# An adaptive-norm layer with a state-space mixer and a routed expert layer: vector copies issued by ScalarE, and the first batch's norm ordered first behind products with the streamed identity

## The chip, the core and the metric

The kernel runs on one core of one Trainium2 chip. The core has five queues of instructions that run in order, each on its own: TensorE (PE in the profile; its weight loads are PEld), VectorE (DVE), ScalarE (ACT), GpSimd (POOL) and SyncE (SP, which here only issues DMAs). The metric is the time of one execution on the device in microseconds (us).

## The reference

The input `x` is 8 batches of 512 tokens with 256 features, all in float32. From a vector `c` per batch six modulation vectors are made; then a mixer and an expert layer are added to `x`:

```python
mod = (silu(c) @ wmod).reshape(8, 6, 1, 256)
sa, ca, ga, sb, cb, gb = (mod[:, i] for i in range(6))
ga, gb = (sign(g) * max(|g|, 0.25) for g in (ga, gb))
h = layernorm(x) * (1 + ca) + sa
x = x + ga * mixer(h)
h = layernorm(x) * (1 + cb) + sb
x = x + gb * experts(h)

def mixer(x):            # 512 inner channels, 16 states, 4 taps
    xz = layernorm(x, gamma, beta) @ W_in.T
    x_part, z = split(xz)
    x_conv = silu(causal_conv4(x_part) + conv_b)
    state_t = state_{t-1} @ A.T + x_part_t @ Bm.T        # over 512 tokens
    y_t = (x_conv_t + state_t @ Cm) * sigmoid(z_t)
    return x + y @ W_out.T

def experts(x):          # 8 experts, hidden size 1024, each token goes to its top one
    probs = softmax(x @ wr + br); p1, p2 = top2(probs)
    return p1 / (p1 + p2) * (gelu(x @ w1[e] + b1[e]) @ w2[e] + b2[e])
```

## The kernel before, in words

**Two parts.** The first handles the mixer and the routing, batch by batch; it writes each token's row (features, statistics, gate) to a DRAM table `xp_d`, whose last 768 columns hold the second half of the modulation vectors for that token's batch, and scatters token numbers sorted by expert into `ids_d`. The second part gathers blocks of up to 256 tokens of one expert, loads that expert's weights, and computes the two expert products (`ph`, `py`).

**The planner.** Nothing is emitted directly. The class `Plan` stands in for the chip's engines: each call is noted with the data it reads and writes, an estimated length and a due time (`nc.due`). Then `order()` repeatedly picks, over all queues, the instruction that could start first, with the due time as the tie-break, and `emit()` writes the instructions in that order. So each engine's order is fixed in the program; an instruction that is placed early and has to wait holds up everything behind it on its engine. A DMA counts as 0.4 us of its issuing queue in these estimates (1.3 on POOL).

**The prologue** has three pieces, all spread over PE, DVE, ACT and POOL:

- `three()` makes one half of the modulation vectors by products with `wm` (tiles `pm`, `pg`), and a chain of seven small DVE operations (copies, `gate`, `mag`). It is called for the first batch alone, broadcast to all partitions (`bc0`), and by `vectors()` for all batches (`mod`, 8 partitions), whose results are stored to DRAM as `mod_d` and `modb_d`. `vectors()` also needs the same vectors with features on partitions (`modT`), from which it makes the router's weights (`rw`, `rg`, `psc`, `wo`, `pr`). Before, `modT` comes from 24 small products `pf` and its own small DVE operations.
- `states()` makes powers of the state matrix (`pa` on PE, copied to `at`), and from them `lt`, `cs` (through `pq`), `wb` (through `pw1`), `lm` (through `pm2`) and `bw` (through `pb`). The copies out of PSUM and between small tiles are on DVE.
- constants: `seen`, `sl_at` and `ex_at` are written by one-element memsets on POOL.

**One batch** is `stage_norm` (load `xt`, load the broadcast vectors `bc` from `mod_d`, two norms with `bn_stats`, `rs` on POOL, `nm` on DVE and `xn` on ACT, then transposes `tp_a` and ACT's copy to `xnT`), `stage_base` (POOL multiplies `h` and `wb_`, transposes `tp_b` to `baseT`), `stage_conv` (`pv`, the carries `pd_0` to `pd_2` over blocks of tokens, four projections `px` to `u` and `sv` on ACT and three taps each on DVE, then SiLU on ACT), `stage_out` (four more projections to `tz`, the state's output `pc`, the residual product `po` and the routing) and `stage_place` (rows to `xp_d`, sorting). `sv`, `u` and `tz` follow the projections; `pc` needs the last carry. PSUM pools: `ps_x` (tag `px`, three buffers), `ps_s` (one), `ps_t` (two), `ps_o` (two).

In `stage_place` the second half of the vectors is copied, 1.5 MB per batch, from `modb_d` to all 512 rows of the batch in `xp_d`. Before, SP issues these copies: two in batch 0, then one in each batch's stage.

```python
            for n in range(b + 1 if b else 0, min(b + 2, B)):
                nc.sync.dma_start(
                    out=xp_d[n * L : (n + 1) * L, OWN:ROW], in_=modb_d[n].partition_broadcast(L)
                )
```

In the profile nearly all instructions carry the line of `Plan.add` that calls the engine (L154 or L159), so they are told apart by their tiles. A product of float32 shows as two instructions (x2).

Of the kernel before, what the change touches and what calls it, by code (L numbers as in the profile page):

```python
# [10 lines left out]
FP = mybir.dt.float32  # L11
I32 = mybir.dt.int32
AF = mybir.ActivationFunctionType
ALU = mybir.AluOpType
# [21 lines left out]
class Plan:  # L36
# [20 lines left out]
    def __init__(self, tc, last=None):  # L57

        self.tc, self.nc = tc, tc.nc
        self.free = {q: last.free[q] if last else 0.0 for q in self.REACH}  # L60
        self.ops, self.touched, self.tiles = [], {}, {}
        self.due, self.also, self.pairing = 0.0, ([], []), 0
        for name in self.QUEUES:
            setattr(self, name, self.Engine(self, name))
# [71 lines left out]
    def add(self, name, op, args, kw):  # L136
# [12 lines left out]
        if queue == "PE" and last and last["queue"] == "PE" and (  # L149
            last["out"] == out.tensor.name or (self.pairing and last["pairing"] == self.pairing)  # L150
        ):

            me = last
            me["calls"].append(lambda: getattr(getattr(self.nc, name), op)(*args, **kw))  # L154
            me["length"] += 0.05 if self.pairing else length
        else:
            me = dict(
                i=len(self.ops), queue=queue, due=self.due,
                calls=[lambda: getattr(getattr(self.nc, name), op)(*args, **kw)],  # L159
                before=set(), after=set(), uses=set(), length=length + (0.3 if small else 0.0),  # L160
                size=0, out=out.tensor.name, pairing=self.pairing,
            )
            self.ops.append(me)
        if op == "activation":
            me["table"] = {AF.Gelu: 1, AF.Silu: 2, AF.Tanh: 2}.get(args[2] if len(args) > 2 else None)
# [25 lines left out]
    def order(self):  # L191
# [18 lines left out]
        done = [0.0] * len(ops)  # L210
        order, table = [], 2

# [12 lines left out]

        while len(order) < len(ops):
            best = None
            for q, l in ready.items():
                for o in l:
# [6 lines left out]
                    if best is None or (at, o["due"]) < best[:2]:  # L236
                        best = (at, o["due"], o)
            assert best is not None, "no buffer for any instruction that could be next"
            at, _, o = best
            table = o.get("table") or table  # L240

            for n in o["uses"] - held:
# [4 lines left out]
            ready[o["queue"]].remove(o)  # L247
            free[o["queue"]] = at + o["length"]
            end = at + o["length"]
            if o["size"]:  # L250
# [39 lines left out]
def adaln_mamba_moe_kernel(  # L290
# [88 lines left out]
    nc.gpsimd.memset(seen, 0.0)  # L379
    for e in range(E):  # L380
        nc.gpsimd.memset(seen[0:1, e : e + 1], float(e * TOK))
    run = cpool.tile([1, E], FP, name="run")


    sl_at = cpool.tile([1, 4, NSLOT], FP, name="sl_at")
    for i in range(NSLOT):
        single = i >= NPAIR
        m = i - NPAIR if single else i
        for q, v in enumerate((
            m, NPAIR + m // 2 if single else m, (m % 2) * P if single else 0,  # L390
            0 if single else NSING,
        )):
            nc.gpsimd.memset(sl_at[:, q, i : i + 1], float(v))

    ex_at = cpool.tile([1, 2, 2 * E], FP, name="ex_at")
    for e in range(2 * E):
        nc.gpsimd.memset(ex_at[:, 0, e : e + 1], float(e % E))
        nc.gpsimd.memset(ex_at[:, 1, e : e + 1], float((e % E) * TOK))

# [32 lines left out]
    with tc.tile_pool(name="wa", bufs=1) as wa, tc.tile_pool(  # L432
# [81 lines left out]
        def vectors():  # L514

            nc.due = 2.5 * PERIOD
            for half, to in ((0, mod_d), (1, modb_d)):
                mod = wa.tile([B, 3, D], FP, name=f"mod{half}", tag="mod")
                three(mod, sT, half, B)
                nc.sync.dma_start(out=to, in_=mod.rearrange("b i d -> b (i d)"))  # L520
            nc.due = 1e6


            pf = ps_o.tile([P, 6, B], FP, name="pf", tag="po")
            for m in range(6):
                w, at_m = (wmh[1], m) if m < 4 else (wmh[0], m)
                for k in range(KD):
                    nc.tensor.matmul(
                        pf[:, m], lhsT=w[:, k, at_m * P : (at_m + 1) * P],
                        rhs=sT[:, k, :], start=(k == 0), stop=(k == KD - 1),  # L530
                    )
            nc.vector.tensor_copy(modT[:, 0:2], pf[:, 0:2])
            nc.vector.tensor_scalar(modT[:, 2:4], pf[:, 2:4], 1.0, None, ALU.add)
            gT = modT[:, 4:6]
            nc.vector.tensor_copy(gT, pf[:, 4:6])
            mT = wa.tile([P, KD, B], FP, name="mT")
            nc.vector.scalar_tensor_tensor(mT, gT, -1.0, gT, ALU.mult, ALU.max)
            nc.vector.tensor_scalar(mT, mT, 0.25, None, ALU.max)
            nc.vector.tensor_scalar(gT, gT, 0.0, 2.0, ALU.is_ge, ALU.mult)
            nc.vector.scalar_tensor_tensor(gT, gT, -1.0, mT, ALU.add, ALU.mult)  # L540

# [51 lines left out]
        def states():  # L593


            for j in range(STEPS - 1):
                pa = ps_s.tile([DS, 2, DS], FP, name="pa", tag="ps")
                for s in range(2):
                    nc.tensor.matmul(
                        pa[:, s], lhsT=at[:, j, 1 - s], rhs=at[:, j, s], start=True, stop=True  # L600
                    )
                nc.vector.tensor_copy(at[:, j + 1], pa)
            i16 = ident[0:DS, 0:DS]
            a3t = wa.tile([DS, DS], FP, name="a3t")
            pa3 = ps_s.tile([DS, DS], FP, name="pa3", tag="ps")
            nc.tensor.matmul(pa3, lhsT=at[:, 0, 1], rhs=at[:, 1, 0], start=True, stop=True)
            nc.vector.tensor_copy(a3t, pa3)
            power = [i16, at[:, 0, 0], at[:, 1, 0], a3t, at[:, 2, 0]]
# [5 lines left out]
            for i in range(CH):  # L614
                for j in range(i + 1):
                    nc.vector.tensor_copy(lt[:, i, j * SP : j * SP + DS], power[i - j])
                nc.vector.tensor_copy(
                    lt[:, i, :].rearrange("p (q r) -> p q r", r=SP)[:, :, DS:],
                    power[i + 1].unsqueeze(1).to_broadcast([DS, CH, DS]),
                )  # L620
# [8 lines left out]
            for i, (l, r) in enumerate((  # L629
# [3 lines left out]
                nc.tensor.matmul(pmo[:, i], lhsT=l, rhs=r, start=True, stop=True)  # L633
            nc.vector.tensor_copy(more[:, 0:5], pmo)
            pm28 = ps_s.tile([DS, DS], FP, name="pm28", tag="ps")
            nc.tensor.matmul(pm28, lhsT=at[:, 4, 0], rhs=more[:, 0], start=True, stop=True)
            nc.vector.tensor_copy(more[:, 5], pm28)
# [8 lines left out]
            nc.vector.tensor_copy(wb[:, :, DS:], pw1)  # L646

# [4 lines left out]
            for j, m in enumerate(gaps):  # L652
                nc.vector.tensor_copy(
                    lx[:, j, :].rearrange("p (q r) -> p q r", r=SP)[:, :, DS:],
# [3 lines left out]
            nc.vector.memset(ix, 0.0)  # L658
            nc.vector.tensor_copy(ix[:, DS:], i16)
            pm2 = ps_s.tile([P, len(gaps), 2 * DS], FP, name="pm2", tag="ps")  # L660
# [3 lines left out]
            nc.vector.tensor_copy(lm, pm2)  # L664

# [11 lines left out]
            nc.vector.memset(bw, 0.0)  # L677
            pb = ps_s.tile([P, KD, DS], FP, name="pb", tag="ps")
            for k in range(KD):
                for j in range(KI):  # L680
# [3 lines left out]
                    )  # L684
            nc.vector.tensor_copy(bw[:, :, 0:DS], pb)

# [227 lines left out]
        def stage_place(t):  # L914
# [11 lines left out]
            )  # L926
            for n in range(b + 1 if b else 0, min(b + 2, B)):
                nc.sync.dma_start(
                    out=xp_d[n * L : (n + 1) * L, OWN:ROW], in_=modb_d[n].partition_broadcast(L)
                )  # L930

# [179 lines left out]

        PERIOD = 36.0
        cs, wb, lm, bw = states()
        rw, rsum, wr2 = vectors()
        for b in range(B):
            nc.due = (b + 3) * PERIOD
            t = stage_norm(b)
            stage_base(t)
            stage_conv(t)
# [284 lines left out]
```

## Time and profile before

| | |
|---|---|
| median of 3 runs | 592.2 us (590.71 to 592.6) |
| profiled execution | 591.06 us, its span on the core 589.4 us |
| PE busy | 555.4 us, 94% of the span |
| DVE, ACT, POOL busy | 358.9, 209.8, 207.9 us |
| granted TensorE clock, mean | 0.975 |
| first product of the batches (`px_0` of batch 0) | starts at 36.7 us |
| last residual product of batch 1 | ends at 122.0 us |
| last residual product of batch 7 | ends at 318.4 us |
| expert layer | to the end; the last `ph` at 573 us |

A row of the order in time gives the start, the length, the engine, the line, the operation, output and inputs with their shapes, how many were grouped, and in square brackets how long the engine was idle before it and what ended that. The DMA issues of SP are rows of SPq; their length is the time that the issue held the queue, not the transfer.

### The profile page before, as it was taken

Reading aid. Unit: us, or ns where it says so; the run is one execution under the profiler, and the core shown is the slowest. Engines: PE = TensorE matmul, PEld = TensorE weight load, DVE = VectorE, ACT = ScalarE, POOL = GpSimd, SP = SyncE. Lnnn points to the kernel's source line nnn. Section 1 sums busy time; section 2 is a strip of 40 time slices with the busy share of each in tenths; the row PEclk is TensorE's granted clock in tenths of the full one; section 3 lists DMA queues with packets and bytes.
Section 4 is the critical chain, followed back from the end, with each engine's and each line's share of the span. In section 5 each row is a group of like instructions: output and inputs, shape, how many; then the busy total and the mean of one; then the engine's idle time right before and its main releaser. Section 6 shows DMA issues by size and latency. Waiting matters only on the chain. (4 is left out here: it accounts for less than half of the span.)

```text
span 589.4 us, 8687 instructions
## 1 busy us (share of the span) xinstructions
PE 555.4 (94%) x2882; PEld 417.4 (71%) x2882; DVE 358.9 (61%) x1087; ACT 209.8 (36%) x404; POOL 207.9 (35%) x338
## 2 busy tenths in 40 slices
PE   5979997999999998999999898999999999999995
PEld 2544752756667573757658787888988988888895
DVE  5879958899796969688585923164243433522312
ACT  2318352635445553533341122213422222332140
POOL 1424270553636154453332420343242222322111
PEclk9869997999999998999999998999999999999999
DMA  7479985421210100001282979998887887786000
GB/s 271 145 189 248 269 243 120 65 64 36 61 41 0 38 1 22 16 0 38 62 271 58 250 176 397 392 407 281 280 272 268 277 254 246 270 289 195 15 18 21
DMA packets 58704, 96.73 MB, mean 164 GB/s; under 512 B 9852, under 2 KB 41854, under 8 KB 58656
## 3 DMA queue, kind: packets, MB, share of 16 engines
q1 hardware_dynamic: 50720, 72.98, 40.8%
q0 software_dynamic: 7936, 23.17, 11.3%
q8 instruction: 24, 0.39, 0.4%
q14 instruction: 24, 0.20, 0.1%
HBM read 86.42 MB, written 22.81 MB: 185 GB/s over the span
## 5 line engine op out<-in xcount | busy, mean ns | idle before, releaser
L159 ACT ACTIVATE gl<-ph,b1t 128x256 f32<-128x256 f32 (+1 forms) x152 | 68.4, 452 | 178.8 <-PE ph L154 144.9
L154 PE MATMUL py<-w2t,gl 128*128 128x256 f32 x476 | 109.1, 381 | 0.0
L154 PEld LDWEIGHTS py<-w2t,gl 128*128 128x128 f32 x476 | 91.2, 192 | 12.6
L159 PE MATMUL ph<-hT,w1t 128*128 128x256 f32 (+1 forms) x304 | 84.1, 358 | 3.2 <-ACT gl L159 1.6
L154 PE MATMUL ph<-hT,w1t 128*128 128x256 f32 (+1 forms) x304 | 84.2, 359 | 0.0
L159 DVE TENSOR_TENSOR ot<-py,b2t 128x256 f32<-128x256 f32 x34 | 14.4, 425 | 112.9 <-PE py L154 112.9
L159 DVE SCALAR_TENSOR_TENSOR sv<-u,pt,sv 128x512 f32<-128x512 f32 x96 | 76.3, 804 | 9.1 <-ACT sv L159 8.8
L159 POOL DMA_INDIRECT out<-ot,ids x36 | 36.2, 1006 | 129.3 <-DVE ot L159 119.7
L159 PE MATMUL px<-xnT,wi 128*128 128x512 f32 x128 | 72.4, 649 | 0.0
L154 PE MATMUL px<-xnT,wi 128*128 128x512 f32 x128 | 68.3, 616 | 0.0
L159 POOL DMA_INDIRECT xg<-xp_d,ids x36 | 39.5, 1097 | 73.1 <-DMA ids<-ids_d 27.4
L159 PEld LDWEIGHTS ph<-hT,w1t 128*128 128x128 f32 x304 | 54.7, 190 | 10.0 <-issue 2.2
L154 PEld LDWEIGHTS ph<-hT,w1t 128*128 128x128 f32 x304 | 55.5, 191 | 6.3
L154 PEld LDWEIGHTS px<-xnT,wi 128*128 128x128 f32 x128 | 25.5, 199 | 32.8 <-issue 32.8
L159 POOL DMA_INDIRECT ids_d<-tok,row x32 | 34.6, 1080 | 35.4 <-DVE row L159 26.3
L159 ACT COPY u<-px 128x512 f32<-128x512 f32 x32 | 18.7, 586 | 58.5 <-PE px L154 58.5
L159 PEld LDWEIGHTS px<-xnT,wi 128*128 128x128 f32 x128 | 22.0, 198 | 18.9 <-issue 16.6
L159 DVE COPY hT<-tp 128x512 f32<-128x512 f32 (+1 forms) x20 | 12.7, 635 | 36.9 <-PE tp L154 28.9
L159 ACT ACTIVATE tz<-px 128x512 f32<-128x512 f32 x32 | 19.1, 596 | 40.0 <-PE px L154 35.1
L159 POOL TENSOR_TENSOR rs<-ve,nhalf 128x4 f32<-128x4 f32 x16 | 19.2, 1203 | 34.8 <-DVE ve L159 33.7
L159 DVE TENSOR_TENSOR hg<-hg,xg 128x256 f32<-128x256 f32 x72 | 29.2, 424 | 1.1
L154 PE MATMUL pc<-v,cs 128*128 128x128 f32 x192 | 26.7, 275 | 0.0
(348 smaller groups left out, 924.6 us busy)
## 6 DMA issues: line engine op xcount, KB each, us to landing
w1t<-in_w SPq DMA_DIRECT2D x19, 1024.0 KB
w2t<-in_w SPq DMA_DIRECT2D x19, 1024.0 KB
xp_d<-modb_d SPq DMA_DIRECT2D x8, 1536.0 KB
xp_d<-xr SPq DMA_DIRECT2D x8, 520.0 KB
xt<-in_x SPq DMA_DIRECT2D x8, 512.0 KB
bc<-mod_d SPq DMA_DIRECT2D x7, 384.0 KB
b2t<-in_b SPq DMA_DIRECT2D x19, 128.0 KB
w<-in_w SPq DMA_DIRECT2D x2, 1024.0 KB
```

Of the source, the lines that this page charges most:

```text
L154: me["calls"].append(lambda: getattr(getattr(self.nc, name), op)(*args, **kw))
L159: calls=[lambda: getattr(getattr(self.nc, name), op)(*args, **kw)],
```

## The change

- **The planner** gets three modes. Up to its time `hold` (24) it prefers, among instructions that can start within 0.3 us of the first, the one due first. Up to `thick` (100) it prefers products that stream much, when PE has streamed little in its last 3.4 us. While `warm` lasts (20) it fills PE's gaps with products of the identity with itself, streamed twice (128x256), whose result `pwarm` nobody reads.
- **Batch 0's norm** (`stage_norm(0)`) is noted first with due time 20, then `states()` and `vectors()`; `stage_base(0)` follows, and `vectors()` may not start before `xnT` of batch 0 is done.
- **`modT`** is read from six transposes of the finished vectors `mod` (tile `pf`) in place of 24 products and their DVE operations. The two calls of `three()` have due times of 36 and 46.8 where 90 stood.
- **The copies in `states()`** (`at`, `a3t`, `lt`, `more`, `wb`, `lx`, `ix`, `lm`, `bw`) go from DVE to ACT; `pw1`, `pm2` and `pb` go from the PSUM pool with one buffer to the one with three.
- **The copies of the vectors** to `xp_d` are all issued by ACT, noted in batch 0's `stage_place` with due time 144. In the order that results, one stands on ACT ahead of `u` of `px_3` of batch 0, six stand between `baseT` of batch 0 and `xnT` of batch 1 (among them `wb`, `lm`, `xn` and a `cs`), and the last stands later, beside `baseT` of batch 1.
- **Constants** come from four iotas into a tile `whole` and a few DVE copies and memsets. SP loads `pt`, `xt` and both `wm` first, and `at` after them.

```diff
+        self.hold, self.thick, self.warm = 0.0, 0.0, None
...
+                if could:
+                    mine = min(could)
+                    if mine[0] < self.hold:
+                        mine = min((c for c in could if c[0] < mine[0] + 0.3), key=lambda c: c[1:3])
+                    if q == "PE" and mine[0] < self.thick:
+                        t, l = mine[0], mine[3]["length"]
+                        lately = sum(
+                            d * max(0.0, b - max(a, t + l - 3.4)) / (b - a) for a, b, d in streamed[-40:]
+                        )
+                        if lately + mine[3]["dense"] < 1800:
+                            dense = [c for c in could if c[3]["dense"] > 900 * c[3]["length"] and c[0] < t + 0.3]
+                            mine = min(dense, key=lambda c: c[1:3]) if dense else mine
...
+            if self.warm and o["queue"] == "PE" and at < self.warm[0]:
+                slow = 2 if at < self.warm[1] else 1
+                n = int(0.8 * (at - free["PE"]) / (slow * self.warm[2]))
+                if n > 0:
+                    order.append(dict(i=-1, at=free["PE"], queue="PE", calls=[self.warm[3]] * n))
+                    fillers += 1
+                length *= slow
...
-    for e in range(E):
-        nc.gpsimd.memset(seen[0:1, e : e + 1], float(e * TOK))
+    nc.vector.tensor_copy(seen[0:1, :], whole[:, 2 * E : 3 * E])
...
-            nc.due = 2.5 * PERIOD
+            pf = ps_o.tile([P, 6, B], FP, name="pf", tag="po")
             for half, to in ((0, mod_d), (1, modb_d)):
+                nc.due = (1 + 0.3 * half) * PERIOD
                 mod = wa.tile([B, 3, D], FP, name=f"mod{half}", tag="mod")
                 three(mod, sT, half, B)
                 nc.sync.dma_start(out=to, in_=mod.rearrange("b i d -> b (i d)"))
+                for m, i in ((0, 1), (2, 0)) if half else ((4, 2),):
+                    for k in range(KD):
+                        nc.tensor.transpose(
+                            pf[:, m + k], mod[:, i, k * P : (k + 1) * P], ident[0:B, 0:B]
+                        )
+            nc.due = 3 * PERIOD
+            nc.vector.tensor_copy(modT, pf)
...
-                nc.vector.tensor_copy(at[:, j + 1], pa)
+                nc.scalar.copy(at[:, j + 1], pa)
...
-            pw1 = ps_s.tile([P, SPAN[0], DS], FP, name="pw1", tag="ps")
+            pw1 = ps_x.tile([P, SPAN[0], DS], FP, name="pw1", tag="px")
...
-            for n in range(b + 1 if b else 0, min(b + 2, B)):
-                nc.sync.dma_start(
+            if b == 0:
+                nc.due = (B / 2) * PERIOD
+                for n in range(B):
+                    nc.scalar.dma_start(
...
+        pwarm = ps_o.tile([P, 2, P], FP, name="pwarm", tag="po")
+        twice = ident.unsqueeze(1).to_broadcast([P, 2, P])
+        plan.hold, plan.thick = 24.0, 100.0
+        plan.warm = (20.0, 7.8, 0.47, lambda: chip.tensor.matmul(
+            pwarm, lhsT=ident, rhs=twice, start=True, stop=True
+        ))
+        nc.due = 20.0
+        t = stage_norm(0)
+        nc.due = 1e6
         cs, wb, lm, bw = states()
+        with nc.wanting(done=[t["xnT"]]):
+            rw, rsum, wr2 = vectors()
+            nc.due = 3 * PERIOD
+            stage_base(t)
```

More of the change, by code (lines that the diff above doesn't have):

```diff
@@ L163, in add @@
             self.ops.append(me)
+        if queue == "PE":
+            n = 1
+            for c in ins[1 if op == "matmul" else 0].shape[1:]:
+                n *= c
+            me["dense"] = me.get("dense", 0) + (2 if op == "matmul" else 1) * n * ins[0].shape[0] / P
         if op == "activation":
@@ L210, in order @@
         done = [0.0] * len(ops)
-        order, table = [], 2
+        order, table, fillers, streamed = [], 2, 0, []
         def may(o):
@@ L224, in may @@
             return at
-        while len(order) < len(ops):
+        while len(order) < len(ops) + fillers:
             best = None
             for q, l in ready.items():
+                could = []
                 for o in l:
@@ L235, in order @@
                         at += 1.3
-                    if best is None or (at, o["due"]) < best[:2]:
-                        best = (at, o["due"], o)
+                    could.append((at, o["due"], o["i"], o))
+                if could:
[10 more added lines that the diff above has]
+                            mine = min(dense, key=lambda c: c[1:3]) if dense else mine
+                    if best is None or mine[:3] < best[:3]:
+                        best = mine
             assert best is not None, "no buffer for any instruction that could be next"
-            at, _, o = best
+            at, _, _, o = best
             table = o.get("table") or table
@@ L247, in order @@
             ready[o["queue"]].remove(o)
-            free[o["queue"]] = at + o["length"]
-            end = at + o["length"]
+            length = o["length"]
+            if self.warm and o["queue"] == "PE" and at < self.warm[0]:
[3 more added lines that the diff above has]
+                    order.append(dict(i=-1, at=free["PE"], queue="PE", calls=[self.warm[3]] * n))
+                    streamed.append((free["PE"], at, 512 * n))
+                    fillers += 1
+                length *= slow
+            if o["queue"] == "PE":
+                streamed.append((at, at + length, o["dense"]))
+            free[o["queue"]] = at + length
+            end = at + length
             if o["size"]:
@@ L379, in adaln_mamba_moe_kernel @@
     nc.gpsimd.memset(seen, 0.0)
-    for e in range(E):
-        nc.gpsimd.memset(seen[0:1, e : e + 1], float(e * TOK))
+    whole = cpool.tile([1, 4 * E + NSLOT], I32, name="whole")
+    for lo, pattern in (
+        (0, [[0, 2], [1, E]]), (2 * E, [[0, 2], [TOK, E]]),
+        (4 * E, [[1, NPAIR]]), (4 * E + NPAIR, [[1, NSING]]),
+    ):
+        n = 1
+        for _, c in pattern:
+            n *= c
+        v = whole[:, lo : lo + n]
+        nc.gpsimd.iota(
+            v.rearrange("o (h e) -> o h e", h=2) if len(pattern) > 1 else v,
+            pattern=pattern, base=0, channel_multiplier=0,
+        )
+    nc.vector.tensor_copy(seen[0:1, :], whole[:, 2 * E : 3 * E])
     run = cpool.tile([1, E], FP, name="run")
     sl_at = cpool.tile([1, 4, NSLOT], FP, name="sl_at")
[L386 to L393, printed above, removed]
+    nc.due = 1e3
+    for q in range(2):
+        nc.vector.tensor_copy(sl_at[:, q, :], whole[:, 4 * E :])
+    nc.gpsimd.memset(sl_at[:, 2:4, :], 0.0)
+    nc.gpsimd.memset(sl_at[:, 3, 0:NPAIR], float(NSING))
+    for m in range(NSING):
+        nc.gpsimd.memset(sl_at[:, 1, NPAIR + m : NPAIR + m + 1], float(NPAIR + m // 2))
+        if m % 2:
+            nc.gpsimd.memset(sl_at[:, 2, NPAIR + m : NPAIR + m + 1], float(P))
     ex_at = cpool.tile([1, 2, 2 * E], FP, name="ex_at")
-    for e in range(2 * E):
-        nc.gpsimd.memset(ex_at[:, 0, e : e + 1], float(e % E))
-        nc.gpsimd.memset(ex_at[:, 1, e : e + 1], float((e % E) * TOK))
+    nc.vector.tensor_copy(ex_at.rearrange("o q e -> o (q e)"), whole[:, 0 : 4 * E])
+    nc.due = 1e6
     NIDS = E * TOK + BLK
@@ L520, in vectors @@
                 nc.sync.dma_start(out=to, in_=mod.rearrange("b i d -> b (i d)"))
[L521 to L540, printed above, removed]
+                for m, i in ((0, 1), (2, 0)) if half else ((4, 2),):
+                    for k in range(KD):
+                        nc.tensor.transpose(
+                            pf[:, m + k], mod[:, i, k * P : (k + 1) * P], ident[0:B, 0:B]
+                        )
+            nc.due = 3 * PERIOD
+            nc.vector.tensor_copy(modT, pf)
             rw = wa.tile([P, KD, 2, B, E], FP, name="rw")
@@ L606, in states @@
             nc.tensor.matmul(pa3, lhsT=at[:, 0, 1], rhs=at[:, 1, 0], start=True, stop=True)
-            nc.vector.tensor_copy(a3t, pa3)
+            nc.scalar.copy(a3t, pa3)
             power = [i16, at[:, 0, 0], at[:, 1, 0], a3t, at[:, 2, 0]]
@@ L615, in states @@
                 for j in range(i + 1):
-                    nc.vector.tensor_copy(lt[:, i, j * SP : j * SP + DS], power[i - j])
-                nc.vector.tensor_copy(
+                    nc.scalar.copy(lt[:, i, j * SP : j * SP + DS], power[i - j])
+                nc.scalar.copy(
                     lt[:, i, :].rearrange("p (q r) -> p q r", r=SP)[:, :, DS:],
@@ L633, in states @@
                 nc.tensor.matmul(pmo[:, i], lhsT=l, rhs=r, start=True, stop=True)
-            nc.vector.tensor_copy(more[:, 0:5], pmo)
+            nc.scalar.copy(more[:, 0:5], pmo)
             pm28 = ps_s.tile([DS, DS], FP, name="pm28", tag="ps")
             nc.tensor.matmul(pm28, lhsT=at[:, 4, 0], rhs=more[:, 0], start=True, stop=True)
-            nc.vector.tensor_copy(more[:, 5], pm28)
+            nc.scalar.copy(more[:, 5], pm28)
             back = [i16, at[:, 2, 1], at[:, 3, 1], more[:, 0], at[:, 4, 1], more[:, 1], more[:, 2],
                     more[:, 5]]
-            pw1 = ps_s.tile([P, SPAN[0], DS], FP, name="pw1", tag="ps")
+            pw1 = ps_x.tile([P, SPAN[0], DS], FP, name="pw1", tag="px")
             for g in range(SPAN[0]):
@@ L645, in states @@
             nc.vector.memset(wb, 0.0)
-            nc.vector.tensor_copy(wb[:, :, DS:], pw1)
+            nc.scalar.copy(wb[:, :, DS:], pw1)
             gaps = [at[:, 5, 0], at[:, 6, 0], more[:, 3], at[:, 7, 0], at[:, 8, 0], more[:, 4]]
@@ L652, in states @@
             for j, m in enumerate(gaps):
-                nc.vector.tensor_copy(
+                nc.scalar.copy(
                     lx[:, j, :].rearrange("p (q r) -> p q r", r=SP)[:, :, DS:],
@@ L658, in states @@
             nc.vector.memset(ix, 0.0)
-            nc.vector.tensor_copy(ix[:, DS:], i16)
-            pm2 = ps_s.tile([P, len(gaps), 2 * DS], FP, name="pm2", tag="ps")
+            nc.scalar.copy(ix[:, DS:], i16)
+            pm2 = ps_x.tile([P, len(gaps), 2 * DS], FP, name="pm2", tag="px")
             for j in range(len(gaps)):
@@ L663, in states @@
             lm = wa.tile([P, len(gaps), 2 * DS], FP, name="lm")
-            nc.vector.tensor_copy(lm, pm2)
+            nc.scalar.copy(lm, pm2)
             wx = wxo[:, 1].rearrange("p (j d) -> p j d", j=KI)
@@ L677, in states @@
             nc.vector.memset(bw, 0.0)
-            pb = ps_s.tile([P, KD, DS], FP, name="pb", tag="ps")
+            pb = ps_x.tile([P, KD, DS], FP, name="pb", tag="px")
             for k in range(KD):
@@ L684, in states @@
                     )
-            nc.vector.tensor_copy(bw[:, :, 0:DS], pb)
+            nc.scalar.copy(bw[:, :, 0:DS], pb)
             return cs, wb, lm, bw
@@ L926, in stage_place @@
             )
-            for n in range(b + 1 if b else 0, min(b + 2, B)):
-                nc.sync.dma_start(
-                    out=xp_d[n * L : (n + 1) * L, OWN:ROW], in_=modb_d[n].partition_broadcast(L)
-                )
+            if b == 0:
+                nc.due = (B / 2) * PERIOD
+                for n in range(B):
+                    nc.scalar.dma_start(
+                        out=xp_d[n * L : (n + 1) * L, OWN:ROW], in_=modb_d[n].partition_broadcast(L)
+                    )
+                nc.due = 3 * PERIOD
             sx = sm.tile([P, NT, E], FP, name="sx")
@@ L1112, in adaln_mamba_moe_kernel @@
         PERIOD = 36.0
+        pwarm = ps_o.tile([P, 2, P], FP, name="pwarm", tag="po")
[6 more added lines that the diff above has]
+        t = stage_norm(0)
+        nc.due = 1e6
         cs, wb, lm, bw = states()
-        rw, rsum, wr2 = vectors()
+        with nc.wanting(done=[t["xnT"]]):
+            rw, rsum, wr2 = vectors()
+            nc.due = 3 * PERIOD
+            stage_base(t)
         for b in range(B):
             nc.due = (b + 3) * PERIOD
-            t = stage_norm(b)
-            stage_base(t)
+            if b:
+                t = stage_norm(b)
+                stage_base(t)
             stage_conv(t)
```

## The prediction

> **What bounds the kernel now.** I read the page's forty slices first, then the table by stage, then the order in time of PE, DVE, ACT and SP up to 125 us.
>
> In the slices PE is full almost everywhere; the gaps are at the head, around 30 us, and around 90 us. The clock row dips there too.
>
> ```profile
> PE   5979997999999998999999898999999999999995
> ...
> PEclk9869997999999998999999998999999999999999
> DMA  7479985421210100001282979998887887786000
> ```
>
> The table by stage (span, PE busy and the count in brackets, weight loads, DVE, ACT, POOL, granted clock, DMA share, GB/s) puts numbers on it:
>
> ```profile
> 0.00:20.00 20.00, 12.92 (x77) 7.76 (x78) 13.21 (x61) 4.65 (x8) 2.85 (x25) 1.00 0.82 294
> 20.00:40.00 20.00, 16.84 (x66) 8.15 (x66) 15.61 (x56) 5.65 (x10) 11.34 (x16) 0.67 0.41 118
> ...
> 80.00:100.00 20.00, 15.27 (x68) 7.32 (x69) 12.03 (x35) 8.89 (x17) 8.04 (x12) 0.88 0.56 170
> ...
> 120.00:160.00 40.00, 38.44 (x199) 24.77 (x199) 34.88 (x102) 19.10 (x34) 19.87 (x32) 1.00 0.17 50
> ```
>
> From 120 us on PE is 96% busy, so the batches are bound by products; the prologue is bound by chains through all engines. Three rows of PE in order of time show the clock's price: the same projection of one 512-column chunk takes 3.7 us after the 3.2 us gap and 1.72 us later (83.86 to 85.58).
>
> ```profile
> 33.30 0.61 PE L159 MATMUL pb<-pt,wxo 128*128 128x16 f32 x2 [3.16 <-DVE more L159]
> ...
> 36.74 2.05 PE L159 MATMUL px<-xnT,wi 128*128 128x512 f32 x2
> 38.58 1.91 PE L154 MATMUL px<-xnT,wi 128*128 128x512 f32 x2
> ...
> 83.86 1.02 PE L159 MATMUL px<-xnT,wi 128*128 128x512 f32 x2
> ...
> 91.74 0.35 PE L159 MATMUL pd<-v,wb 128*32 128x128 f32 x1 [2.57 <-DVE v L159]
> ```
>
> The hole at 90 us begins on DVE, which waits for a tile of x that SP issued at 77.46 behind the copies of the vectors. These are the copies on SP, with how long each issue held SP:
>
> ```profile
> 90.01 0.75 DVE L159 BATCH_NORM_STATS2 st<-xt 128x6 f32<-128x256 f32 x2 [7.96 <-DMA xt<-in_x]
> ...
> 35.34 1.26 SPq L159 DMA_DIRECT2D xp_d<-modb_d  x2
> ...
> 37.33 5.19 SPq L159 DMA_DIRECT2D xp_d<-modb_d  x1
> ...
> 42.56 7.60 SPq L159 DMA_DIRECT2D xp_d<-modb_d  x1
> ...
> 50.21 8.28 SPq L159 DMA_DIRECT2D xp_d<-modb_d  x1
> ```
>
> The first three go at about 0.6 us each, the fourth holds its queue 5.2 us, the later ones 7.6 to 8.3 us: the queue takes about three and a half copies, then SP waits for the wire. On SP this cost nothing directly. That is the row to remember.
>
> **The change part by part.** My mark is the last product of batch 1's residual (`po`), which ends at 122.0 before. Beyond it both kernels' PE orders repeat the same pattern, three rows apart, in a stage 96% busy, and the experts follow from the last batch. So a shift at the mark is carried to the end one for one.
>
> *Head.* Six products with the streamed identity run before `pm`. Each is like `pg`, 256 columns, 0.83 to 0.9 us at the slow clock, 5.2 us in all, while `wm` is still in flight (PE waited for it until 7.93). They cost nothing unless `wm` lands before about 7 us; then at most one of them, 0.9. `pm` then takes 1.9 instead of 3.7. The first norm is ordered first: before, `nm` was ready at 9.1 (POOL's `rs`) but stood on DVE behind the copy of `pm` until 12.4, and the second `nm` (POOL ready 21.95) stood until 24.3 behind a copy of `at` that waited for PE. With 2.08 for `xn` and 2.45 for the two multiplies, `xnT` is done at about 23, before at 30.0: 7 us.
>
> The Trainium skill (TensorE: Matmul & The Clock Gate, "What's actually happening") says that the clock opens after some 3.4 us of busy time and closes after an idle window; the rows above show both ends, and no row shows 256-column fillers doing it. If they did not, `pm` would be back at 3.7.
>
> *What is put in front of the projections.* The 24 small `pf` products (17.15 to 19.99, 2.8 us) become 6 transposes of the finished vectors, at most 0.16 each by `tp` rows, 1 us. But these wait for DVE's chain of seven operations on `mod`, and `px_0` and `px_1` stand behind them on PE. The chain costs 2.6 us by its rows, and its SBUF-only operations wait for POOL's 2.4 us multiplies (before: `mag` 2.33, `lt` 2.32 beside POOL's `h`). POOL has three of them from about 22 to 29.5, so the first `mod` is ready near 30.5 and `px_0` starts near 31 (before 36.74). The second `mod` shares a buffer and waits for the first's store (26.15 to 27.79 before, 1.6): near 33.5, then `pv` 1.0, and `px_1` near 35 (before 42.40).
>
> *To the first carry `pd_0`.* From 34: six projections 10.3, `pv` 1.0, `wo`'s transposes and `tp_b` 1.8, `pw1` 2.0, `pm2` 1.4, small ones 1.0 = 17.5, and some 2 us for ACT, which now has DVE's copies too (about 40 of 0.15 to 0.3; the nearest ACT row, `gt` 128x4, is 0.21, so 8 us, beside 17 us that ACT idled in the head waiting for `nm`). `pd_0` at 53.5, before at 52.44. But `px_4` to `px_6`, `tp_b` and `psc` (6.5) are done and two `pq` (2.0) are not: 4.5 more work in 1.1 more time, 3.4 gained.
>
> *The copies on ACT.* Their due time is 144 us, but the written order fills gaps: one copy stands before `u` of `px_3`, six stand between `baseT` and `xnT` of batch 1, one later. Queued on ACT behind the six: `wb`, `lm`, `xn` and `xnT` of batch 1. PE's next rows need just these: `pd_0` (`wb`), `pd_1` (`lm`), `tp_a` (`xn`), `px_0` of batch 1 (`xnT`), and behind `px_0` stand `pr` and all `pc` of batch 0. No row shows a DMA issued by ACT. Bounds: six times 0.4 to 0.6 (free queue), or SP's run, 35.34 to 58.5, 23 us for six. I take SP's run less the 0.65 MB that lay ahead of it (2.6 us at 250 GB/s): 20.5, as it is the same transfer on the same wire. ACT's last SiLU of batch 0 waits for DVE's twelfth tap: from 34.3, twelve taps at 0.75, three multiplies `h` at 1.22, and 2.5 of small ones, so near 50. `tz` and two `baseT` follow and end near 52.4, so the last issue ends near 73 and `px_0` starts at 74. Free, it would start near 61 (DVE's `nm` at 56, `xn` 2.1, `tp_a` 0.9, `xnT` 1.45).
>
> The Trainium skill (DMA: Bandwidth & Descriptors, "Issuing engines are not separate DMA queues") calls the issuing sequencer's time usually small beside the transfer. The rows of 5.2 to 8.3 us speak against it here; by the page the start would be 61 and the sum the first rival's.
>
> *Rest to the mark.* By rows: `pr` 1.7, eight `pc` at 0.89, nine `px` at 1.72, eight `po` at 2.23, two `pv` 2.0, carries 1.3, `pk` 0.5, five half transposes 2.2: 48.2. One cold projection after the hole adds 1.9, idle 1.5 (as in 120 to 160). SP no longer holds the tile of x, so the hole at 90 (2.6 + 1.3 + 0.5 idle, 3.2 of cold projections) goes. 74 + 48.2 + 3.4 = 125.6, 3.6 later than 122.0. What is late next is DVE (18.1 of 20 us in 100 to 120).
>
> *At nothing:* 116 one-element memsets on POOL (0.09 each) become a few iotas; POOL is 35% busy and waits for others. Without that cover, 10 us of POOL fall away, a gain at most. Three PSUM tiles move to another pool with three buffers: hidden by the `px` stream; if not, one eviction of 0.6.
>
> **The sum.** The profiled execution took 591.06 (span 589.4). 591.1 + 3.6 = 594.7. The median shown, 592.2, is 1.1 above that execution, so 595.8.
>
> **The rivals.** *ACT is not held (faster).* Place: the six issues after `baseT`. If ACT's queue swallows them, the start is 61, the mark 61 + 48.2 + 1.5 = 110.7, 11.3 earlier; DVE gives some back, so 8 to 11: 581 to 585. It decides at a hold of 17 us: a start at 70.4 puts the mark at 122.0. For: ACT's queue starts empty. Against: SP's rows. 0.22.
>
> *Held, but shorter.* If `baseT` ends at 49.5 and the copies run at the wire's 250 GB/s (6.3 each), the hold ends at 49.5 + 4.6 + 12.6 = 66.7, the start is 68, the mark 119.6: 590. 0.25, a quarter of it no change.
>
> *More than held.* DVE, late by the hole, meets two batches' taps, and tiles of x share the wire: 4 to 8 more, 599 to 603. 0.11. That the copies move late, as their due says, is excluded by the written order.
>
> **How the numbers follow.** The forecast, 593 to 598, has 0.42, of which 0.05 is no change. Within 0.3% (1.8 us) is about what a measurement of this kernel can't tell from none. Faster: 0.22 + 0.19 = 0.41. Same: 0.06 + 0.05 = 0.11. Slower: 0.37 + 0.11 = 0.48. Signs are split, so the range spans both: 580 to 603; the forecast's own is 593 to 598.
>
> **What would show it.** Right: ACT rows of 5 to 8 us for `xp_d<-modb_d`, a PE gap of 8 us or more before batch 1's first `px`, released by ACT `xnT`; `xnT` of batch 0 by 24; no DVE wait for `xt` near 90. Wrong: ACT's issues all under 1 us, or the first `px` of batch 1 before 69.

## The result and the profile after

The changed kernel is slower: median 600.4 us (599.11 to 601.61, 4 runs) beside 591.46 us (589.59 to 592.6, 4 runs) of the kernel before, a ratio of 1.0159 with an interval of 1.0132 to 1.0186. The profiled execution took 599.11 us, its span 597.4 us, at a mean granted clock of 0.964. The forecast was 595.8: the side and the mechanism were right, the loss is 8.9 us and not 3.6. Ratios here compare fast runs alone; two of the runs of experiment 3, at 598.7 and 601.87 us, were slow and are left out.

The slices of the page (each digit is a fortieth of the span, 14.9 us) show that the head is full and the hole near 90 us is gone. A deeper hole, one digit of 0, stands at 60 to 75 us, and the clock row falls ahead of it.

```profile
PE   8998099999999999999989988989999999999996
...
PEclk9697589999999999999999989999999999999999
DMA  8359993355110101010371979999786887786000
```

The table by stage (span, then PE, weight loads, DVE, ACT and POOL with counts in brackets, granted clock, DMA share, GB/s) prices it: in 60 to 80 us PE works 6.42 of 20 us at half the clock while the wire is 99% busy; no engine works much. From 80 us on PE is full.

```profile
60.00:80.00 20.00, 6.42 (x24) 3.90 (x24) 1.70 (x2) 5.86 (x11) 4.74 (x4) 0.51 0.99 283
80.00:100.00 20.00, 20.00 (x115) 15.10 (x115) 16.33 (x34) 6.15 (x11) 4.63 (x14) 1.00 0.68 188
```

ACT in order of time says who is waited for. Rows of ACTq are DMA issues; their length is the time that the issue held ACT's queue.

```profile
39.73 0.56 ACTq L160 DMA_DIRECT2D xp_d<-modb_d  x1
...
48.71 0.48 ACTq L160 DMA_DIRECT2D xp_d<-modb_d  x1
...
49.36 0.51 ACTq L160 DMA_DIRECT2D xp_d<-modb_d  x1
...
49.91 1.18 ACTq L160 DMA_DIRECT2D xp_d<-modb_d  x1
...
51.13 3.21 ACTq L160 DMA_DIRECT2D xp_d<-modb_d  x1
...
54.55 11.76 ACTq L160 DMA_DIRECT2D xp_d<-modb_d  x1
...
66.33 6.99 ACTq L160 DMA_DIRECT2D xp_d<-modb_d  x1
73.37 1.45 ACT L160 ACTIVATE xnT<-tp_a,pt 128x512 f32<-128x512 f32 x2 [16.24 <-issue]
```

The issues cost little until the fifth; the sixth holds ACT for 11.76 us and the seventh for 6.99. `xnT` of batch 1 stands behind them: ACT is idle for 16.24 us before it, with "issue" as the releaser, so the profile shows nothing else that it waited for. PE's row follows:

```profile
74.20 2.08 PE L160 MATMUL px<-xnT,wi 128*128 128x512 f32 x2 [13.58 <-ACT xnT L160]
```

### The profile page after: what moved, and what is told of

It reads as the page before. It is cut to its first block, busy times and chain, and to the rows that moved or that the text cites. A ratio compares the mean times of both kernels' runs of the same rounds, so it can differ in the third digit from the quotient of the medians.

```text
span 597.4 us, 8590 instructions
## 1 busy us (share of the span) xinstructions
PE 560.0 (94%) x2878; PEld 420.1 (70%) x2878; DVE 349.5 (59%) x1050; ACT 214.8 (36%) x439; POOL 209.9 (35%) x238
## 4 chain that ended last, share of the span: by engine, by line
PE 51%; DMA 22%; DVE 14%; issue 5%; SPq 2%; ACTq 2%; POOL 2%; ACT 1%; POOLq 0%; DVEq 0%
DMA xg<-xp_d,ids 10%; PE py L155 10%; PE po L155 8%; DVE sv L160 7%; PE ph L160 6%; PE ph L155 6%; DMA ids_d<-tok,row 5%; PE px L160 4%; PE px L155 4%; DVE h L160 3%; DMA ids<-ids_d 3%; PE pc L155 3%; PE po L160 3%; DMA w1t<-in_w 2%; ACTq L160 2%
## 5 line engine op out<-in xcount | busy, mean ns | idle before, releaser
L155 PEld LDWEIGHTS py<-w2t,gl 128*128 128x128 f32 x476 | 90.4, 190 | 12.7 <-issue 0.5
L160 PE MATMUL px<-xnT,wi 128*128 128x512 f32 x128 | 69.3, 624 | 13.6 <-ACT xnT L160 13.6
L160 DVE SCALAR_TENSOR_TENSOR sv<-u,pt,sv 128x512 f32<-128x512 f32 x96 | 69.8, 741 | 2.1 <-ACT sv L160 2.0
L155 PE MATMUL px<-xnT,wi 128*128 128x512 f32 x128 | 66.3, 600 | 0.0
L160 POOL DMA_INDIRECT ids_d<-tok,row x32 | 36.1, 1127 | 33.0 <-DVE row L160 21.1
L155 PEld LDWEIGHTS px<-xnT,wi 128*128 128x128 f32 x128 | 24.6, 192 | 31.2 <-issue 30.6
L160 PEld LDWEIGHTS px<-xnT,wi 128*128 128x128 f32 x128 | 21.5, 192 | 31.3 <-issue 15.8
L160 ACT COPY u<-px 128x512 f32<-128x512 f32 x32 | 18.7, 584 | 60.8 <-PE px L155 60.8
L160 DVE COPY hT<-tp 128x512 f32<-128x512 f32 (+1 forms) x20 | 12.7, 634 | 34.8 <-PE tp L155 34.8
L160 DVE TENSOR_TENSOR xr<-po,h 128x256 f32<-128x256 f32 x32 | 13.5, 422 | 29.7 <-PE po L155 29.7
L160 POOL TENSOR_TENSOR h<-h,bc 128x1024 f32<-128x1024 f32 x8 | 19.1, 2386 | 24.7 <-ACT xn L160 24.5
```

## The experiments

Each ratio is against runs of the kernel before on the same chip. "Mark" is, as in the prediction, the end of batch 1's last residual product `po`: 122.2 us before, 127.8 us after.

**1. Copies back on SyncE.** The changed kernel with the old loop of copies.

```diff
-            if b == 0:
-                nc.due = (B / 2) * PERIOD
-                for n in range(B):
-                    nc.scalar.dma_start(
...
+            for n in range(b + 1 if b else 0, min(b + 2, B)):
+                nc.sync.dma_start(
...
```

> The changed kernel with the copies of the vectors issued by SP again, as before (seven in a row from about 35 us, one later); all else of the change stays. Theory, the hold: the changed kernel loses its time because six issues hold ACT's queue from 48.7 to 73.3 us. Then the PE gap of 13.6 us before batch 1's first projection goes and this projection starts near 60 instead of 74.2. The tile of x of batch 4 is again behind the copies, so DVE waits for it some 5 to 8 us around 85. Time 586 to 594, at least 6 under the changed kernel. Rival, the head: ACT's extra copies and the new order of the prologue cost the time whoever issues the copies. Then 598 to 602.

Measured: 597.76 us, ratio 1.0096 (1.0066 to 1.0126). The hole at 60 to 80 us is gone (`px_0` of batch 1 starts at 58.76), and the expectation was missed all the same. Rows of SP, DVE and PE of this kernel:

```profile
37.77 30.03 SPq L160 DMA_DIRECT2D xp_d<-modb_d  x7
...
93.42 0.43 DVE L160 BATCH_NORM_STATS2 st<-xt 128x6 f32<-128x256 f32 x1 [12.10 <-DMA xt<-in_x]
...
97.73 0.42 PE L160 MATMUL pd<-v,lm 128*32 128x128 f32 x1 [10.78 <-DVE v L160]
```

Seven copies hold SP for 30 us, and the tile of x behind them comes no earlier (DVE goes on at 93.4 us, before at 90.0), while the work that needs it is now ready sooner: DVE waits 12.1 us where it waited 7.96. The mark is at 123.5. So seven copies issued in a row leave the new head no gain, neither on SP, ahead of the loads of x, nor on ACT, ahead of `xnT`.

**2. Only the copies on ACT.** The kernel before, with the changed kernel's block of copies and nothing else of the change.

> The kernel before with one part of the change: the copies of the vectors are issued by ACT in batch 0's stage. In the written order six of them stand on ACT between sv and u of batch 0's first two projections, near 41 us. Theory, the hold: ACT is held from about 41 to about 65 us, rows of 5 to 12 us among its issues, PE runs out of PSUM buffers for projections and has a gap of 15 us or more; the wait of 8 us for x near 85 goes. Time 598 to 606, slower than before. Rival: issues by ACT are short or harmless, and only the wait for x goes: 584 to 590.

Measured: 608.46 us, ratio 1.0286 (1.0257 to 1.0314), a little over the range. The copies alone lose 16 us, more than the whole change, at another place, since the old order puts other work behind them:

```profile
40.67 20.06 ACTq L159 DMA_DIRECT2D xp_d<-modb_d  x5
60.88 6.74 ACTq L159 DMA_DIRECT2D xp_d<-modb_d  x1
...
62.09 2.07 PE L159 MATMUL pq<-cmt,lt 16*128 16x512 f32 x2 [12.18 <-ACT sv L159]
...
68.99 2.07 PE L159 MATMUL pq<-cmt,lt 16*128 16x512 f32 x2 [4.83 <-ACT sv L159]
```

**3. One copy per batch on ACT.** The changed kernel, two copies in batch 0 and one in each later batch, each behind the batch's rows `xr`.

```diff
+            for n in range(b + 1 if b else 0, min(b + 2, B)):
+                with nc.wanting(done=[xr]):
+                    nc.scalar.dma_start(
...
```

> The changed kernel with the same eight copies on ACT, but one for each batch, ordered behind that batch's finished rows (two in the first), so that never more than two are outstanding. Theory, the hold: all issues take under 1 us, batch 1's first projection starts near 60, no wait for x near 85. Time 578 to 585, under the kernel before by 6 to 13. Rival, the head: ACT's queue still carries eight issues and DVE's copies, so the loss stays: 595 to 602.

Measured: ratio 0.998 (0.9953 to 1.0008), no difference that shows, so the expectation was missed, though all its issues take 0.5 to 0.6 us each and `px_0` of batch 1 starts at 59.4 us. The mark came at 109.5, 12.7 us earlier than before, and batch 7 still ended 9 us earlier; then nearly all of the gain was lost in one wait: the last copy is on the wire together with the first expert's weights.

```profile
318.26 1.22 PE L160 MATMUL ph<-hT,w 128*128 128x256 f32 x2 [8.55 <-DMA w<-in_w]
```

**4. An eighth of each copy in place.** The changed kernel with the orders of PE and ACT kept: ACT's issues carry 64 of 512 rows, SP issues the other 448, one per batch behind `xr`.

> The changed kernel with the same order of instructions on ACT and PE, but each copy that ACT issues carries one eighth of its rows (64 of 512); SP issues the other seven eighths, one copy per batch, behind that batch's rows. Theory, the hold is paced by the bytes in flight: ACT's issues each take under 1 us, batch 1's first projection starts at 60 to 62, time 578 to 586. Rival, the hold is a fixed cost of an issue by ACT or a wait that only looks like one: the issues keep 3 to 12 us and the time stays at 596 or more.

Measured: 587.65 us, ratio 0.9938 (0.9916 to 0.9961). All issues on ACT hold it 0.48 to 0.61 us, `px_0` of batch 1 starts at 59.35, PE is busy 20.00 of 20 us from 60 to 80, and the mark is 112.9. The time lies 1.7 us over its range: again `ph` waits for weights (4.45 us until 313, 2.56 until 355). With the same orders, the two kernels are 127.8 - 112.9 = 14.9 us apart at the mark and 600.4 - 587.65 = 12.7 in the medians. The mark is the cleaner price of the hold, since the waits for weights of experiment 4 come behind it.

**5 and 6. Two copies per batch in batches 0 to 3**, behind `xr`, on ACT and on SP.

```diff
+            for n in range(2 * b, min(2 * b + 2, B)):
+                with nc.wanting(done=[xr]):
+                    nc.scalar.dma_start(        # nc.sync in the second
...
```

> The changed kernel, its copies on ScalarE two per batch behind the rows of the batch in batches 0 to 3, so never more than two outstanding and all done near 190 us, 100 us before the first expert's weights are asked for near 296. Theory (the hold of ScalarE's queue by copies issued back to back is what costs; without it the head's gain of some 12 us at the end of batch 1 reaches the end): no hole on TensorE between 60 and 80 us, no wait of ph for weights near 300, 577 to 583. Rival (the end is set by the transition to the experts, whatever the batches gain): 587 to 591, with the gain seen at the last batch's residual and gone behind it.

> As the two per batch on ScalarE, but issued by SyncE. Theory (what matters is how many copies are outstanding at once, not which engine issues them): within 2 us of that kernel, 577 to 584. Rival (SyncE's loads of x stand behind the copies again): DVE waits for xt as in the run with the copies back on SyncE, 588 to 594.

Measured: 584.55 us, ratio 0.9919 (0.9892 to 0.9946), and 584.83 us, ratio 0.992 (0.9889 to 0.995). `px_0` of batch 1 starts at 59.62 and 58.71, the marks are 109.8 and 109.7, and no `ph` waits for the first expert's `w`. No issue is held as in the changed kernel: on ACT each takes 0.5 to 0.7 us, and on SP the longest row, two issues together, is this one:

```profile
124.08 2.28 SPq L160 DMA_DIRECT2D xp_d<-modb_d  x2
```

Which engine issues makes no difference that shows; where the copies stand and how many follow each other does. ("Never more than two outstanding" doesn't hold to the letter: the copy that ACT issued at 97.48 landed 27.3 us later, after the next two had been issued.) Both beat both kernels. The first lies some 1.5 us over its range, between its two theories; of the 12.3 us at the mark, 9.9 are left at batch 7 (308.5 beside 318.4), 8.8 at the end of the profiled execution (582.23 beside 591.06) and 5.2 in the medians. Some of the rest is lost to the weights of later experts: `ph` waits for `w1t` until 351 us in the first (2.64 us), and in the second for `b1t`, which lands last, until 330 us (4.77).

**7. The kernel before with two copies per batch on SP.**

> The kernel before, its copies still on SyncE but two per batch behind the rows of batches 0 to 3; nothing else of the change. Theory: the hole near 90 us (DVE waits 8 us for xt behind the copies; 2.6 + 1.3 + 0.5 of idle TensorE and some 3 of cold projections) goes, 4 to 8 us earlier: 584 to 588; the rest of the difference to the changed kernel with copies two per batch is what the order of the head gains. Rival (xt is late for another reason, the loads' place in SyncE's order): 590 to 593.

Measured: 586.74 us, ratio 0.9964 (0.9934 to 0.9993). DVE's wait for `xt` is gone. The twelve runs go with the granted clock: seven took 584.5 to 586.9 us with a mean clock of 0.984 to 0.988, five took 589.0 to 590.4 us with 0.971 to 0.976; the profiled one is of the second group. It spends 40 to 60 us at a clock of 0.71 (0.98 in the profile of before) and ends at the mark where the kernel before did. But the thirty runs of the kernel before on this chip go with the clock in the same way: the two at 0.984 and 0.986 took 586.4 us, and the eight at 0.971 to 0.976 took 588.8 to 591.5. At a like clock the means of the two kernels are less than 1 us apart. So this kernel ran at the higher clock more often, seven times of twelve beside two of thirty; whether the missing hole brought that or something else in the head, and what the hole itself was worth, is not shown.

**8. No products with the streamed identity.** The kernel of experiment 5 with the fillers left out and the order kept.

> As the two per batch on ScalarE, with the products with the streamed identity left out and everything else in the same order. Theory (they only open the clock for pm, and the head behind it waits for the norm's chain on DVE and ScalarE): pm takes 3.7 instead of 2.5 us and the time rises by 0 to 2. Rival (the clock of the whole head hangs on them, pa, pm2 and the first projections included): 3 to 5 more.

Measured: 586.13 us, ratio 0.9934 (0.9907 to 0.9961); the intervals of 5 and 8 overlap. `pg` ends at 11.6 us instead of 10.3, and the mark comes 1.3 us later too: that is what the fillers are worth there, and the medians can't tell it from none.

**9 and 10. Five and six whole copies in place.** The orders of PE and ACT are kept; before `xnT` of batch 1 five (six) copies are whole, and the remaining two (one) carry 16 rows. SP issues the rest in batch 3.

```diff
+                    k = L if n < 6 else 16      # 7 in the second
+                    part = (xp_d[n * L : n * L + k, OWN:ROW], modb_d[n].partition_broadcast(k))
...
```

> The changed kernel with its orders on TensorE and ScalarE kept, but only five whole copies stand on ScalarE before xnT of batch 1 (seven in the changed kernel); the other two carry 16 of 512 rows there, and SyncE issues their rest in batch 3. Theory (the queue takes some four copies, then each further one waits for the wire; in the changed kernel the seven issues held 0.56, 0.48, 0.51, 1.18, 3.21, 11.76 and 6.99 us): the last whole issue ends near 54.5, in time for xn; px_0 of batch 1 at 60, the last residual product of batch 1 near 110, 583 to 588. Rival (the hold is shared evenly by all copies, 24.6 us over seven): two copies less give 7 us back, px_0 at 67, 590 to 594.

> As the run with five copies in place, with a sixth, which is held. Theory: it holds ScalarE for 11.8 us until 66.3, px_0 of batch 1 starts near 67.5, the last residual product of batch 1 ends near 121, as in the kernel before (122), and the time is 589 to 594; so this one copy costs 5 to 7 us against the run with five. Rival (evenly shared): 3.5 us later than with five.

Measured: 590.28 us, ratio 1.0005 (0.9982 to 1.0029), and 595.18 us, ratio 1.0108 (1.0052 to 1.0163). Both of my expectations failed, and the rows of the first show why (here the rows of 53.88 and 64.51 are the small issues):

```profile
50.32 3.35 ACTq L971 DMA_DIRECT2D xp_d<-modb_d  x2
53.88 10.60 ACTq L971 DMA_DIRECT2D xp_d<-modb_d  x1
64.51 1.30 ACTq L971 DMA_DIRECT2D xp_d<-modb_d  x1
65.86 1.44 ACT L160 ACTIVATE xnT<-tp_a,pt 128x512 f32<-128x512 f32 x2 [9.39 <-issue]
```

An issue of 16 rows, a thirty-second of a copy, is held 10.60 us, as long as the whole sixth copy of the second kernel (10.48); there the small seventh is held 7.84. Of the five copies in the first kernel the one issued at 40.17 had landed after 12.6 us, just before the hold began; the next, issued at 48.26, landed at 61.1, during it. The rival's 590 to 594 for five copies came true, but not for its reason: the hold is not shared evenly; nearly all of it lies in the issue after the fifth copy.

**11. Narrow copies in place.** The orders kept, ACT's issues with all 512 rows but 96 of 768 columns; SP copies the rest, two batches at a time.

> The changed kernel with its orders on TensorE and ScalarE kept, each copy on ScalarE with all its 512 rows but 96 of 768 columns; SyncE copies the other 672 columns, two batches at a time behind the rows of batches 0 to 3. Theory (the bytes on the wire pace the issues, not the number of rows): all issues on ScalarE under 1.5 us, px_0 of batch 1 near 60, 583 to 588. Rival (the number of rows fills and paces the queue): issues of several us as in the changed kernel, px_0 near 74, 596 to 602.

Measured: 583.78 us, ratio 0.991 (0.9883 to 0.9937); `px_0` of batch 1 at 60.11. Yet two issues are far over the 1.5 us that I expected, and one is near it:

```profile
50.65 3.24 ACTq L973 DMA_DIRECT2D xp_d<-modb_d  x1
54.58 1.43 ACTq L973 DMA_DIRECT2D xp_d<-modb_d  x1
56.05 3.05 ACTq L973 DMA_DIRECT2D xp_d<-modb_d  x1
```

The fifth issue is held 3.24 us here, with an eighth of the bytes, and 3.21 in the changed kernel; with an eighth of the rows (experiment 4) it takes 0.61. So the number of rows fills the queue, and with fewer bytes a full queue stays full for less time (the sixth and seventh issue: 1.43 and 3.05 us here, 11.76 and 6.99 in the changed kernel).

**12. Five whole copies and nothing behind them.** As experiment 9 without the two small issues.

> As the run with five copies in place, without the two small ones of 16 rows: six copies are left on ScalarE (five ahead of xnT of batch 1, one later), SyncE issues the last two whole in batch 3. Theory (in the run with five copies the first small issue was held 10.60 us although it had 16 rows: with the queue full, any issue, whatever its size, waits until an earlier copy has left it; the fifth whole copy itself still goes in): the fifth issue ends near 54, nothing holds ScalarE, px_0 of batch 1 starts near 60, the last residual product of batch 1 ends near 113, 583 to 588. Rival (the fifth whole copy is what held ScalarE, and the 10.6 us were its own rows going in): a hold of some 10 us stays, px_0 near 66, 589 to 592.

Measured: 585.37 us, ratio 0.9893 (0.9856 to 0.9929). The fifth copy goes in. Its issue holds ACT 3.41 us, which costs PE 1.22 us (`pd` waits for `lm`), and `xnT` waits for nothing. Rows of ACT, then of PE:

```profile
50.01 1.12 ACTq L160 DMA_DIRECT2D xp_d<-modb_d  x1
51.17 3.41 ACTq L160 DMA_DIRECT2D xp_d<-modb_d  x1
54.62 0.32 ACT L160 COPY lm<-pm 128x192 f32<-128x192 f32 x1 [3.87 <-PE pq L160]
...
58.27 1.43 ACT L160 ACTIVATE xnT<-tp_a,pt 128x512 f32<-128x512 f32 x2
...
54.99 0.42 PE L160 MATMUL pd<-v,lm 128*32 128x128 f32 x1 [1.22 <-ACT lm L160]
...
60.80 2.08 PE L160 MATMUL px<-xnT,wi 128*128 128x512 f32 x2
```

Between 9 and 12 stand two issues of 16 rows, 48 KB each (and 16 rows each in SP's late copies), and 0.9893 became 1.0005, some 6.6 us; the two ratios come from different chips, the starts of `px_0` are 5.9 us apart. With five copies, five and two small ones, six and a small one, and seven ahead of `xnT`, `px_0` of batch 1 starts at 60.8, 66.7, 73.1 and 74.2, and the ratios are 0.9893, 1.0005, 1.0108 and 1.0159.

## Why the prediction was right or wrong, point by point

- **The head: right.** `pm` ends at 9.4, `xnT` of batch 0 at 23.4 (said: 23), `px_0` at 29.7 (31), `px_1` at 33.5 (35), `pd_0` at 51.5 (53.5). The streamed identity opens the clock: `pwarm` is busy from 1.83 to 7.3, and the second half of `pm` runs at full speed, 1.02 us; without them (experiment 8) `pm` starts with a pass of 2.04 us. First the rows of the changed kernel, then those of experiment 8:

```profile
1.83 5.49 PE L1158 MATMUL pwarm<-ident 128*128 128x256 f32 x12 [1.83 <-POOL prio L160]
7.11 1.45 PE L160 MATMUL pm<-wm,s 128*128 128x512 f32 x2
8.39 1.02 PE L155 MATMUL pm<-wm,s 128*128 128x512 f32 x2
```
```profile
7.28 2.04 PE L160 MATMUL pm<-wm,s 128*128 128x512 f32 x2 [7.28 <-DVE ve L160]
9.12 1.58 PE L155 MATMUL pm<-wm,s 128*128 128x512 f32 x2
```

The clock column of the profile reads 1.00 there in both, so only these lengths tell. From them I estimate that the clock opened some 6 us after the first filler, and without fillers some 3 us after `pm` began. The rule of the Trainium skill (TensorE: Matmul & The Clock Gate, "What's actually happening") which the prediction cited agrees in kind: its 3.4 us of busy time lie between the two.
- **The copies on ACT: right in place; right in the end by luck, since two errors cancel.** I said that `baseT` ends at 52.4 and the last issue near 73. `baseT` ended at 50.8 and the issues ran from 48.71 to 73.3, 24.6 us, not 20.5. `px_0` of batch 1 started at 74.20 (said: 74). The page of the Trainium skill that calls an issue's time usually small (DMA: Bandwidth & Descriptors, "Issuing engines are not separate DMA queues") would have put it at 61; that is what experiments 4, 5, 11 and 12 show (59.4 to 60.8), where no copy, smaller ones or only five stand ahead of `xnT`.
- **The rivals.** I priced the free case at 581 to 585, 8 to 11 us earlier, with the mark at 110.7. The mark was priced well: in experiments 5, 6 and 11 it lies between 109.7 and 112.7, in 12 at 114.2. The end was not: their 583.8 to 585.4 us fall into the range, but the kernel before took 589.8 us on two of those chips and 592.25 on the third, so they gain 5.0 to 6.9 us. The shorter hold (an end at 66.7) did not come: it ended at 73.3. The measured 600.4 us lies in the range of the rival "more than held" (599 to 603), but not for its reason: from 74.2 us to the mark PE waits for DVE once, 0.5 us.
- **Step that failed: "Rest to the mark", 51.6 us.** It took 53.56 (74.20 to 127.76). From one start to the next on PE: projections 18.2 where the sum had 17.4 (the cold one took 3.6 as priced, those beside the carries 1.8 to 2.0 each, not 1.72), `pr` 2.6 for 1.7, since the clock was still low and `pr` ran cold as well as the projection, `pv` 2.7 for 2.0, transposes 2.8 for 2.2; only the idle time was smaller than allowed (0.5 for 1.5). So the mark came 5.6 us later than before, not 3.6. The hole at 90 us went, as said. These are `pr` in the changed kernel, the clock beside it (PE busy with the count, clock, DMA share, GB/s), and `pr` before:

```profile
77.78 0.53 PE L160 MATMUL pr<-rg,wxo 128*128 128x64 f32 x2
78.10 2.42 PE L155 MATMUL pr<-rg,wxo 128*128 128x64 f32 x14
```
```profile
76.00:80.00 4.00, 4.00 (x16) 0.56 1.05 300
```
```profile
59.97 0.33 PE L159 MATMUL pr<-rg,wxo 128*128 128x64 f32 x2
60.14 1.73 PE L154 MATMUL pr<-rg,wxo 128*128 128x64 f32 x14
```

- **Step that failed: "a shift at the mark is carried to the end one for one".** Through the batches it holds: batch 7 ends 5.8 us later. Then 2.2 us are added, and the profiled execution is 8.05 us longer. In windows that begin with the experts, PE has the same work in both kernels, and 2 us more idle time in the changed one (82.00 - 77.35 = 4.65 before, 84.00 - 77.38 = 6.62 after):

```profile
318.00:400.00 82.00, 77.35 (x363) 66.66 (x362) 41.23 (x151) 19.28 (x43) 27.79 (x32) 0.98 0.94 311
```
```profile
324.00:408.00 84.00, 77.38 (x359) 65.95 (x359) 40.92 (x146) 19.18 (x42) 27.84 (x27) 0.98 0.94 303
```

Two of its waits are these:

```profile
345.69 1.17 PE L160 MATMUL ph<-hT,w1t 128*128 128x256 f32 x2 [2.41 <-ACT gl L160]
...
395.20 0.30 PE L160 MATMUL tp<-ident,hg 128*128 128x128 f32 x1 [1.26 <-DVE hg L160]
```

The written order of the experts is not the same in the two kernels either: the transposes of gathered rows stand ahead of products that they followed before. From batch 7's last `po` to the end of the span, the profiles of the three kernels with the old head have 270.4 to 271.0 us. Nine with the new head have 271.4 to 273.5; experiments 3 and 4, whose late copies meet the weights, have more. That the order is the cause is argued, not shown: no run changed it alone, and each figure is from one execution.
- **The sum.** 594.7 was said for the profiled execution, 599.11 measured: 2 from the rest to the mark, 2.4 from the carry. The median lies 1.3 above the profiled execution (said: 1.1). That makes 4.6 of the 5.3 us between the loss of 8.9 and that of 3.6; the other 0.7 is the median of the kernel before, 591.46 with a fourth run where 592.2 was shown.
- **What hid the gain.** With the copies two per batch, the mark comes 12 us earlier than before (experiment 5); each placement that loses by it has a wait of its own: DVE for x (copies early on SP, 10.8 us of PE), ACT's queue (all on ACT, 13.6 us), or the first expert's weights (spread to batch 6, 8.6 us).

## What to carry to other kernels

In this kernel a DMA issue cost its engine half a microsecond only while the queue had room. So count the copies that are issued in a row, and look at what stands behind the last one on the issuing engine, small issues included. Large background copies did best two per batch, behind work that is done anyway, and finished before the next stage asked for the wire; then the engine that issued them hardly mattered. And when a term is to be carried from an early stage to the end, price the next stage's start by itself: its order may differ too.

## What the runs showed of the hardware that was not expected

- Behind five copies of 512 rows on ACT, an issue of only 16 rows was held 10.60 us (experiment 9) and, behind a sixth copy, 7.84 us (experiment 10). What frees the queue in such steps isn't settled; the runs show that a thirty-second of the rows did not shorten the wait (10.60 us beside 10.48 for a whole copy).
- The queue fills by rows: 512 rows of 384 bytes held the fifth issue as long (3.24 us) as 512 rows of 3 KB (3.21), and 64 rows of 3 KB not at all (0.61).
- ACT's issues run ahead of its arithmetic: the issue at 48.71 starts beside a SiLU that starts at 48.70, and that at 54.55 beside `xn`, which runs to 56.7. Only what stands behind the held issue waits.
- The clock fell while PE was still busy: `pd` by `lm` took 0.42 us at 54.75, where the same product took 0.27 at 106.56, in a stretch of thin products and gaps under 1 us, ahead of the long one. From 52 to 56 us the granted clock is 0.53 with PE busy 3.25 of 4 us. The head shows it without gaps: from 16 to 20 us PE is busy throughout, with `pb` (16 columns) and `pq` (16 rows) above all, at a clock of 0.50. That thin products are the cause is argued, not shown.
